# A graph layer on one core: the edge network's first product as eight small ones, some gathered rows moved to ScalarE's queue, eleven more picked tiles, another setup and end

## The chip, the cores and the metric

The kernel runs on one core of one Trainium2 chip. The metric is device time in microseconds (us). Before the change it is 1521.2 us, the median of three runs (1520.66 to 1521.42).

## What is computed

The input is a graph of N = 6250 nodes and E = 200000 edges, sorted by target node. Every edge takes the 64 features of its source node and two small vectors. Cut to what matters, the reference is:

```python
w = jax.nn.silu(edge_attr @ W1 + b1) @ W2 + b2                  # E x 32 -> E x 64 -> E x 9
h_src = features[src]                                           # a row of 64 per edge
msg = jnp.einsum('ef,em,fmg->eg', h_src, edge_sh * w, W_tp)     # E x 64
agg = jax.ops.segment_sum(msg, dst, num_segments=N) / jnp.sqrt(AVG_DEG)
emb = jax.nn.silu(c_noise[:, None] @ Wn1 + bn1) @ Wn2 + bn2     # gamma and beta of a node
gamma, beta = jnp.split(emb, 2, axis=-1)
x = layernorm(x + agg * (1.0 + gamma) + beta)
```

## The kernel before

Edges are cut into tiles of 128 (one edge per partition), and 16 tiles make a group; there are 98 groups, the last with 11 tiles. The main loop (L603 to L651) has one iteration i for each group. The order of the instructions on every engine is the order in which the program is written out (`tc.manual_schedule()`, L600), so an instruction that waits holds up all that is written behind it for the same engine.

**The rows of source nodes** come in three ways. For most tiles GpSimd issues one indirect DMA per tile (`gather`, L89, issued at L91), six groups ahead (AHEAD, seven buffers). The last three or four tiles of a group are "picked" instead (`picked`, L50, and `pick`, L463): the whole of x lies in the core's memory as two fp32r parts (`xs`), VectorE makes one-hot matrices of the row numbers (`hots`, L460), TensorE multiplies (14 products of 128x448 per tile, L475), and VectorE selects and sums (L484, L486). 355 tiles are picked, 3 in a group where 3g mod 8 is below 3 and 4 otherwise. In 16 groups (SPG) the first tile's 128 rows are fetched one by one by DMAs of SyncE's queue (`load_rows`, L98; L101 loads eight row numbers into registers, L106 issues one DMA per row, 22 rows in an iteration).

**The edge network**: `hidden(g)` (L398) makes the first layer of 2048 edges with two products of 64 rows by 128 columns by 512 (L403), each against a block-diagonal weight, into the PSUM tile p1 of two banks; one Silu (L411) reads all 1024 columns. `second(g)` (L415) makes the second layer with four 32-column products of 256 (L420) into the PSUM tile with the tag "s". `weights(g)` (L425) transposes the result (L430), multiplies (L436) and lays it out for eight target windows (`a`, L442).

**Sums**: `windows(g)` (L494) multiplies each tile's rows by its a (32 records at L504), and ScalarE copies the results from the PSUM tiles pz to zt with eight copies (L514). `project(q)` (L530), in odd iterations, multiplies two groups by W_tp (L543) into a PSUM tile pt that has p1's tag and so its place; `turn` transposes it back (L549), and `halves` reads it with ScalarE (L524) and VectorE (L525). `place` (L554) adds to nodes (L559), with a carry copied by ScalarE (L565); `bring` (L572, L576) and `finish_nodes` (L667 to L684) close 256 nodes in every fourth iteration (i mod 4 = 3), with ten operations on VectorE and a square root on ScalarE (L680). `gate` (L353) reads gamma and beta of 128 nodes from the PSUM tile "s" in iterations up to 50 (L355, L356).

The order within iteration i is: gather(i+6), loads, rows of SPG, keys(i+2) (the row numbers copied by ScalarE, L454), pick(i+1, 0) with the parts of `nodes(i)` and two one-hots strewn in, hots(i+2, 2 and 3), hidden(i+2), second(i+1), windows(i), project in odd iterations, pick(i+1, 1) with weights(i+1) and turn strewn in, picks 2 and 3. [...]

Of the kernel before, what the change touches and what calls it, by code (L numbers as in the profile page):

```python
# [15 lines left out]
P = 128  # L16
N, F, M, D, H, E = 6250, 64, 9, 32, 64, 200000
NJ = 49
# [13 lines left out]
SPR = 22  # L32
EPS = 1e-5
# [16 lines left out]
def picked(g):  # L50

    return Q - (3 * g % 8 < 3)
# [7 lines left out]
def gnn_resnorm_kernel(ctx: ExitStack, tc: tile.TileContext, x, src, dst, dst_row, ea, sh, cn,  # L60
# [18 lines left out]
    with ExitStack() as fast:  # L79
# [9 lines left out]
        def gather(g):  # L89
            hs[g] = gath.tile([P, KB, F], F32, tag="hs", name=f"hs{g}")  # L90
            hs_dma[g] = [nc.gpsimd.indirect_dma_start(  # L91
                out=hs[g][:, t - g * KB, :], out_offset=None, in_=x,
                in_offset=bass.IndirectOffsetOnAxis(ap=src_i[:, t:t + 1], axis=0))
                for t in range(g * KB + (g in SPG), g * KB + tiles(g) - picked(g))]

        src_r = keep.tile([len(SPG), P], I32)

        def load_rows(g, e0):  # L98
            for e in range(e0, min(e0 + SPR, P), 8):
                n = min(8, min(e0 + SPR, P) - e)  # L100
                _, vs = nc.values_load_multi_w_load_instructions(  # L101
                    src_r[SPG.index(g):SPG.index(g) + 1, e:e + n], engines=[mybir.EngineType.SP],
                    min_val=0, max_val=NPAD - 1,
                    skip_runtime_bounds_check_because="src is below N, as for the gathers")
                for k in range(n):
                    nc.sync.dma_start(hs[g][e + k:e + k + 1, 0, :], x[bass.ds(vs[k], 1), :])  # L106
# [27 lines left out]
        def setup(temp):  # L134
# [4 lines left out]
            for q in range(4):  # L139
                nc.sync.dma_start(w1bd[q * D:(q + 1) * D, (q % 2) * H:(q % 2 + 1) * H], w1)  # L140
            nc.sync.dma_start(src_i[:, AHEAD * KB:], src[:, AHEAD * KB:])
            xb_r = xb.rearrange("p j f -> p (j f)")
            row_i = xb_r[0:1, 0:NBLK * KB].bitcast(I32)
            nc.scalar.dma_start(row_i, dst[0:1, :])
            first_i = temp.tile([NBLK, KB], I32)
            nc.scalar.dma_start(first_i, dst[0].rearrange("(g k) -> g k", k=KB))
            cn_j = temp.tile([NJ, P], F32)
            nc.scalar.dma_start(cn_j, cn)
            for s in range(2):
                nc.scalar.dma_start(b1c[s * H:(s + 1) * H, :], b1.unsqueeze(1))  # L150
# [3 lines left out]
            for h0, h1 in ((0, 2), (2, 4), (4, 7)):  # L154
                nc.scalar.dma_start(xk[:, h0:h1, :], x_v[:, h0:h1, :])
            load(0)
            for s in range(2):
                nc.sync.dma_start(w2p[s * H:(s + 1) * H, s * M:(s + 1) * M], w2)
            nc.sync.dma_start(dst_i, dst)
# [14 lines left out]
            one = temp.tile([1, 1], F32)  # L174
            nc.vector.memset(one, 0.0)
            one_o = temp.tile([1, 1], F32)
            nc.scalar.activation(one_o, one, AF.Silu)
            row_f = xb_r[0:1, NBLK * KB:2 * NBLK * KB]
            nc.scalar.copy(row_f, row_i)
            first_t = temp.tile([NBLK, KB], F32)  # L180
            nc.scalar.copy(first_t, first_i)
# [5 lines left out]
            nc.vector.tensor_add(ident2, ident[:, 0:F], ident[:, F:P])  # L187
            zero = temp.tile([P, 1], F32)
            nc.vector.memset(zero, 0.0)
            for k in range(2):  # L190
                nc.vector.memset(ht[k][H:H + 1], 1.0)
            nc.vector.memset(wtc2[F:P, 4], 0.0)
            ones1 = temp.tile([1, P], F32)
            nc.vector.memset(ones1, 1.0)
            nc.vector.memset(eps, EPS)
            nc.vector.tensor_copy(nk, nk_i)
            nc.vector.tensor_copy(wi, n_i[:, 0:W])
            nc.vector.tensor_copy(li, n_i[:, 0:J])


            zt_r = zt.rearrange("p a c k w -> p (a c k w)")
            s_f, kp, kh, rest, t0, t1 = [zt_r[:, k * C:(k + 1) * C] for k in range(6)]
            ti = [t.bitcast(I32) for t in (t0, t1)]
            s_f = s_f.rearrange("p (g k) -> p g k", k=Q)
            nc.vector.tensor_copy(s_f[:, 0:NBLK - 1, :],
                                  src_i.rearrange("p (g k) -> p g k", k=KB)[:, 0:NBLK - 1, KB - Q:])
            nc.vector.tensor_copy(s_f[:, NBLK - 1, :], src_i[:, NT - Q:NT])
            s_f = s_f.rearrange("p g k -> p (g k)")
            nc.vector.tensor_scalar(ti[0], s_f, 2675.0, None, op0=ALU.mult)
            nc.vector.tensor_scalar(ti[0], ti[0], 17, None, op0=ALU.logical_shift_right)  # L210
            nc.vector.tensor_copy(kp, ti[0])
            nc.vector.scalar_tensor_tensor(rest, kp, -float(J * J), s_f, op0=ALU.mult, op1=ALU.add)
            nc.vector.tensor_scalar(ti[1], rest, 37.0, None, op0=ALU.mult)
            nc.vector.tensor_scalar(ti[1], ti[1], 8, None, op0=ALU.logical_shift_right)
            nc.vector.tensor_scalar(kh, ti[1], float(P), None, op0=ALU.mult)
            kf = s_f
            nc.vector.tensor_add(kf, kp, kh)
            for c0 in range(0, C, P):
                n = min(P, C - c0)
                p_kt = psum.tile([P, P], F32, tag=("s", "r")[c0 // P % 2], name=f"p_kt{c0}")  # L220
                nc.tensor.transpose(p_kt[0:n], kf[:, c0:c0 + n], ident)
                kt = t1[:, c0 // 2:c0 // 2 + P // 2].bitcast(F16)
                nc.scalar.copy(kt[0:n], p_kt[0:n])
                nc.sync.dma_start(kd[c0:c0 + n, :], kt[0:n])
            nc.vector.scalar_tensor_tensor(jl, kh, -float(J) / P, rest, op0=ALU.mult, op1=ALU.add)
            hidden(0, act=False)
            load_keys(0)
            load_keys(LB)
            for c in range(KB // 4):
                for s in range(2):  # L230
                    q = c * D + s * M
                    nc.sync.dma_start(b2c[q:q + M, :], b2.unsqueeze(1))


            rel_v = rel.rearrange("p (a b c) -> p a b c", a=2, b=2)
            dst_v = dst_i.rearrange("p (a b c) -> p a b c", a=2, b=2)
            row_v = row_f.rearrange("p (a b c) -> p a b c", a=2, b=2)

            def base(a_):
                p_b = psum.tile([P, 2, KB * P // 4], F32, tag="p1", name=f"p_b{a_}")  # L240
                for b_ in range(2):
                    nc.tensor.matmul(p_b[:, b_, 0:NBLK * KB // 4], ones1, row_v[:, a_, b_, :], start=True, stop=True)
                nc.vector.tensor_sub(rel_v[:, a_], dst_v[:, a_], p_b[:, :, 0:NBLK * KB // 4])


# [8 lines left out]
            nc.vector.tensor_copy(pw, pw_i)  # L254

            def ids():
                p_nid = psum.tile([P, NBLK], F32, tag="s", name="p_nid")
                nc.tensor.matmul(p_nid, sel, first_f, start=True, stop=True)
                nc.vector.scalar_tensor_tensor(nid, p_nid, pw, lo, op0=ALU.add, op1=ALU.subtract)

            def between(h):

                if h == 0:
                    p_f = psum.tile([KB, NBLK], F32, tag="s", name="p_f")
                    nc.tensor.matmul(p_f, first_t, ident[0:NBLK, 0:NBLK], start=True, stop=True)
                    nc.scalar.copy(first_f, p_f)
                elif h == 1:
                    keys(0)
                    hots(0, 0, Q)
                elif h == 3:  # L270
                    p_cn = psum.tile([P, NJ], F32, tag="s", name="p_cn")
                    nc.tensor.matmul(p_cn, cn_j, ident[0:NJ, 0:NJ], start=True, stop=True)
                    cn_s = temp.tile([P, NJ], F32)
                    nc.scalar.copy(cn_s, p_cn)
                    nc.sync.dma_start(cn_d, cn_s)
                    nc.sync.dma_start(wn1c, wn1.rearrange("o h -> h o"))
                    nc.sync.dma_start(bn1c, bn1.unsqueeze(1))
                    gate_load(0)
                    nc.sync.dma_start(wn2a[0:H, :], wn2)
                    nc.sync.dma_start(wn2a[H:H + 1, :], bn2.unsqueeze(0))  # L280
                    for q in range(2):
                        n = (M + 1 - q) // 2
                        nc.sync.dma_start(wtc2[q * F:(q + 1) * F, 0:n, :], wtp[:, q:M:2, :])
                    load(LB)
                    with nc.allow_non_contiguous_dma(reason="2048 words, once"):
                        nc.sync.dma_start(src_r, src[:, SPG[0] * KB:NBLK * KB:6 * KB].rearrange("p g -> g p"))
# [572 lines left out]
```

## Time and profile before

| | us |
|---|---|
| median of the runs | 1521.2 |
| the profiled execution | 1521.78 |
| its span, first to last instruction | 1519.9 |
| GpSimd's 1192 indirect DMAs: first and last start | 2.92 and 1493.22 |
| TensorE busy, of these products of the picks (L475) | 1438.0, 1090.6 |
| VectorE busy | 1135.4 |
| ScalarE busy | 526.1 |
| windows of group 0, 48, 52, 60, 96 begin (timeline, L504) | 55.8, 766.7, 825.8, 940.3, 1493.7 |

The profiled execution took 0.58 us more than the median. In the group rows of the profile a line shows the source line, the engine, the operation, the tile written and the tiles read, their shapes and the count; behind the bar are the busy time, the mean duration of one in ns, and the idle time ahead of these instructions with what ended it. In the timeline a line shows the start, the time covered (of several merged instructions the whole stretch), the engine and the instruction. PE is TensorE, PEld its weight loads, DVE VectorE, ACT ScalarE, POOL GpSimd, and SPq SyncE's queue.

### The profile page before, as it was taken

The numbers are of one execution on the slowest core, as the hardware profiler recorded it, in microseconds if no ns is written. First come the engines' busy times: TensorE is split into PE (matmuls) and PEld (weight loads), VectorE is DVE, ScalarE is ACT, GpSimd is POOL, SyncE is SP. The second block draws the span as 40 slices with busy tenths as digits, with TensorE's granted clock in tenths as the row PEclk, the third lists the DMA queues.
The fourth block names the chain that finished last, engine by engine and source line by source line (L and its number), as shares of the span: only waits on it lengthen the run. The fifth ranks groups of instructions, "written<-read, shape, count | busy, mean of one in ns | idle before, by whom it ended". The sixth has DMA issues, their size and how long they took to land.

```text
span 1519.9 us, 34363 instructions
## 1 busy us (share of the span) xinstructions
PE 1438.0 (95%) x10810; PEld 1192.7 (78%) x10810; DVE 1135.4 (75%) x1987; ACT 526.1 (35%) x1335; POOL 1129.3 (74%) x1201
## 2 busy tenths in 40 slices
PE   4998999999999999999999999989998998999995
PEld 2787888888888788888888888878777887878784
DVE  5686777877877878777777877768677777687773
ACT  4223342433423333332423424424233333333331
POOL 7777777777777777777777777777777777777772
PEclk9999999999999999999999999999999999999997
DMA  6422232222222222222322222222222222222210
GB/s 171 95 56 63 54 76 53 64 59 70 65 56 72 58 63 71 60 63 54 74 59 55 72 52 63 71 54 61 53 72 53 59 55 71 52 55 59 73 29 15
DMA packets 90939, 96.16 MB, mean 63 GB/s; under 512 B 37161, under 2 KB 51451, under 8 KB 90748
## 3 DMA queue, kind: packets, MB, share of 16 engines
q0 software_dynamic: 38144, 39.14, 13.4%
q1 hardware_dynamic: 51842, 53.09, 12.1%
q8 instruction: 88, 1.44, 0.4%
q10 hardware_dynamic: 762, 1.64, 0.3%
q14 instruction: 103, 0.84, 0.2%
HBM read 92.04 MB, written 1.73 MB: 62 GB/s over the span
## 4 chain that ended last, share of the span: by engine, by line
PE 57%; POOL 18%; issue 9%; SPq 5%; DMA 5%; DVE 4%; ACT 2%; DVEq 0%; POOLq 0%; ACTq 0%
PE px L475 41%; POOL hs L91 18%; PE pz L504 5%; DMA hs<-in_x_dram,src_i 4%; PE p L403 3%; SPq L106 3%; PE pt L543 3%; PE p L420 2%; SPq L101 2%; PE p L430 1%; PE ps L559 1%; PE ps L589 0%; ACT st L411 0%; DVE hot_k L460 0%; DVE xm L484 0%
## 5 line engine op out<-in xcount | busy, mean ns | idle before, releaser
L91 POOL DMA_INDIRECT hs<-in_x_dram,src_i x1192 | 1128.0, 946 | 364.3 <-issue 330.7
L475 PE MATMUL px<-xs,hot_k 128*128 128x448 f32 x4970 | 1090.6, 372 | 9.4 <-DVE xs L294 8.8
L475 PEld LDWEIGHTS px<-xs,hot_k 128*128 128x128 f32 x4970 | 896.8, 189 | 93.9 <-issue 10.9
L484 DVE SCALAR_TENSOR_TENSOR xm<-li,jl,px 128x448 f32<-128x448 f32 x355 | 240.3, 677 | 203.6 <-PE px L475 202.0
L460 DVE TENSOR_TENSOR hot_k<-pk,nk 128x896 fp32r<-128x896 f32 x355 | 370.6, 1082 | 3.1 <-ACT pk L454 3.1
L411 ACT ACTIVATE st<-p,b1c 128x1024 f32<-128x1024 f32 x98 | 109.5, 1118 | 405.4 <-PE p L403 405.1
L486 DVE TENSOR_REDUCE hs<-xm 128x64 f32<-128x448 f32 x355 | 220.1, 620 | 12.2
L514 ACT COPY zt<-pz 64x160 f32<-64x160 f32 (+2 forms) x784 | 213.5, 272 | 40.6 <-PE pz L504 28.0
L504 PEld LDWEIGHTS pz<-a,hs 128*64 128x64 f32 x3126 | 110.2, 142 | 68.1 <-issue 61.2
L504 PE MATMUL pz<-a,hs 128*64 128x72 f32 x3126 | 124.6, 234 | 27.0 <-DMA hs<-in_x_dram,src_i 11.5
L442 DVE TENSOR_TENSOR a<-oh,p 128x1152 f32<-128x1152 f32 x98 | 132.7, 1354 | 3.3
L436 DVE TENSOR_TENSOR p<-p,sh 128x72 f32<-128x72 f32 x196 | 47.0, 240 | 100.9 <-ACT rt L546 45.2
L403 PE MATMUL p<-ea,w1bd 64*128 64x512 f32 x392 | 113.3, 655 | 0.0
L565 ACT COPY carry<-ps 128x128 f32<-128x128 f32 x48 | 12.8, 266 | 273.4 <-PE ps L559 273.4
L420 PEld LDWEIGHTS p<-st,w2p 128*32 128x32 f32 x784 | 15.8, 108 | 83.2 <-issue 39.0
L420 PE MATMUL p<-st,w2p 128*32 128x256 f32 x784 | 63.5, 396 | 7.8 <-DVE xb L356 7.8
L680 ACT ACTIVATE var<-var,eps 128x2 f32<-128x2 f32 (+1 forms) x25 | 7.4, 295 | 179.2 <-DVE var L679 179.2
L543 PE MATMUL pt<-zt,wtc 128*64 128x128 f32 x960 | 64.3, 281 | 2.6 <-ACT zt L514 1.7
L543 PEld LDWEIGHTS pt<-zt,wtc 128*64 128x64 f32 x960 | 55.0, 142 | 3.8 <-ACT zt L514 1.9
L454 ACT CAST pk<-kr 128x384 f32<-128x384 f16 (+1 forms) x98 | 53.8, 549 | 2.2 <-DMA kr<-kd 2.2
L430 PE MATMUL p<-ident,p2s 128*128 128x128 f32 x196 | 53.3, 273 | 0.0
L403 PEld LDWEIGHTS p<-ea,w1bd 64*128 64x128 f32 x392 | 30.0, 187 | 28.7 <-issue 28.0
(122 smaller groups left out, 529.0 us busy)
## 6 DMA issues: line engine op xcount, KB each, us to landing
hs<-in_x_dram SPq DMA_DIRECT2D x2048, 0.2 KB
ea<-in_ea_dram SPq DMA_DIRECT2D x49, 512.0 KB
hs<-in_x_dram,src_i POOLq DMA_INDIRECT x1192
kr<-kd SPq DMA_DIRECT2D x49, 256.0 KB
sh<-in_sh_dram SPq DMA_DIRECT2D x49, 144.0 KB
cb<-cn_d SPq DMA_DIRECT2D x12, 128.0 KB
out_dram<-o SPq DMA_DIRECT2D x24, 64.0 KB
gam<-in_x_dram ACTq DMA_DIRECT2D x2, 448.0 KB
```

The lines of the kernel that those rows point to most:

```text
L91: hs_dma[g] = [nc.gpsimd.indirect_dma_start(out=hs[g][:, t - g * KB, :], out_offset=None, in_=x, in_offset=bass.IndirectOffsetOnAxis(ap=sr ...
L403: nc.tensor.matmul(p1[:, i, :], w1bd[i * 64:(i + 1) * 64, :], e[i * 64:(i + 1) * 64, :], start=True, stop=True)
L411: nc.scalar.activation(st[g], p1_t.pop(g), AF.Silu, bias=b1c)
L420: nc.tensor.matmul(p2[g][c * D:(c + 1) * D, 0, :].rearrange("p (i e) -> p i e", i=2), w2p, s[:, :, c * P:(c + 1) * P], start=True, stop=True)
L442: nc.vector.tensor_mul(a[g], oh_t.pop(g)[:, :, None, :].to_broadcast([P, KB, M, W]), sw.unsqueeze(3).to_broadcast([P, KB, M, W]))
L460: nc.vector.tensor_tensor(hot_k[g, t], pk_t[g][:, t, None, :].to_broadcast([P, J, P]), nk.unsqueeze(2).to_broadcast([P, J, P]), op=ALU.is_ ...
L475: nc.tensor.matmul(px.rearrange("p f l -> p (f l)"), hot_k[g, t][:, h, :], xs[i][:, h].rearrange("p f l -> p (f l)"), start=(h == 0 and i ...
L484: nc.vector.scalar_tensor_tensor(xm, li[:, None, :].to_broadcast([P, F, J]), jl[:, c:c + 1], px, op0=ALU.is_equal, op1=ALU.mult)
L486: nc.vector.tensor_reduce(hs[g][:, tiles(g) - q + t, :], xm, AX.X, ALU.add)
L504: mm = nc.tensor.matmul(pz[v * F:(v + 1) * F, k // 2].rearrange("p m w -> p (m w)"), hsg[:, k0 + k, :], ag[:, k0 + k].rearrange("p m w -> ...
L514: nc.scalar.copy(z[h * F:(h + 1) * F, 0:5 - h, k0 + v:k0 + n:2, :].rearrange("p m k w -> p k m w"), pz[v * F:(v + 1) * F, 0:(n + 1 - v) // ...
L543: nc.tensor.matmul(pt[h * F:(h + 1) * F, 0, 0:P], wtc2[:, c, :], z[h][:, c], start=(c == 0), stop=(c == 4))
```

## The change

1. **First layer.** `hidden(g)` makes eight products of 32 rows by 64 columns by 256 (four row parts q, two column parts s) in place of two. They go to four banks: the two of p1, half used, and the two of pz, which `windows` uses too. Three Silu instructions (256, 256 and 512 columns) read them. hidden(i+2) moves from behind pick(i+1, 0) to behind pick(i+1, 1). L420 and L436 read their operands in the new arrangement; their counts and sizes stay.
2. **ScalarE's rows.** In seven groups (16, 28, ... 88; ACG) the first tile's 128 rows come one by one from ScalarE's queue, 11 in each of the twelve iterations before, behind hidden(i+2); the indirect DMA of that tile goes.
3. **Picks.** `picked` is 3 where g mod 4 = 0 and in the last group, 4 otherwise: 366 tiles. 1174 indirect DMAs are left.
4. **Setup.** x is loaded first and in four pieces; it is split with one ScalarE copy per part in place of two; the row numbers of groups 0 and 1 are spread by a product on TensorE, and only those of the later groups take the way through DRAM; most of the other small steps come after the first picks.
5. **End.** The last three picks, project and place come ahead of the last windows; the last group's windows run in reverse order with four PSUM banks, and ScalarE and VectorE share the copies; the store of finished nodes is issued at the start of the next iteration.

The diff, cut to its core:

```diff
 def picked(g):
-    return Q - (3 * g % 8 < 3)
+    return Q - (g % 4 == 0 or g == NBLK - 1)
...
+ACG = range(16, NBLK, 12)
+ACR = 11
...
-                for t in range(g * KB + (g in SPG), g * KB + tiles(g) - picked(g))]
+                for t in range(g * KB + (g in SPG or g in ACG), g * KB + tiles(g) - picked(g))]
...
+            if g in SPG:
+                eng, kind, n1, to = nc.sync, mybir.EngineType.SP, SPR, hs[g][:, 0, :]
+            else:
+                eng, kind, n1, to = nc.scalar, mybir.EngineType.Activation, ACR, hs_r[ACG.index(g) % 2]
...
                 for k in range(n):
-                    nc.sync.dma_start(hs[g][e + k:e + k + 1, 0, :], x[bass.ds(vs[k], 1), :])
+                    eng.dma_start(to[e + k:e + k + 1, :], x[bass.ds(vs[k], 1), :])
...
-        def hidden(g, act=True):
+        def hidden(g):
             e = ea_t.pop(g)
-            p1 = psum.tile([P, 2, KB * P // 4], F32, tag="p1", name=f"p1_{g}")
-            for i in range(2):
-                nc.tensor.matmul(p1[:, i, :], w1bd[i * 64:(i + 1) * 64, :], e[i * 64:(i + 1) * 64, :],
-                                 start=True, stop=True)
...
-            nc.scalar.activation(st[g], p1_t.pop(g), AF.Silu, bias=b1c)
+            p1 = psum.tile([P, 2, 4 * P], F32, tag="p1", name=f"p1_{g}")
+            bank = [p1[:, i, 0:2 * P] for i in range(2)]
+            bank += [psum.tile([P, 2 * P], F32, tag="pz", name=f"p1_{g}_{i}", bufs=2) for i in range(2)]
+            for q in range(4):
+                eq = e[q * D:(q + 1) * D, :].rearrange("p (c s e) -> p s c e", s=2, e=P)
+                for s in range(2):
+                    nc.tensor.matmul(bank[q][s * H:(s + 1) * H].rearrange("p (c e) -> p c e", e=P),
+                                     w1bd[q * D:(q + 1) * D, (q % 2) * H:(q % 2 + 1) * H], eq[:, s],
+                                     start=True, stop=True)
+            st[g] = work.tile([P, 4, 2 * P], F32, tag="st", name=f"st{g}")
+            nc.scalar.activation(st[g][:, 2], bank[2], AF.Silu, bias=b1c)
+            nc.scalar.activation(st[g][:, 3], bank[3], AF.Silu, bias=b1c)
+            nc.scalar.activation(st[g][:, 0:2], p1[:, :, 0:2 * P], AF.Silu, bias=b1c)
...
-                if i + 2 < NBLK:
-                    hidden(i + 2)
                 if i + 1 < NBLK:
                     second(i + 1)
-                if i < NBLK - 2:
+                if i < NBLK - 1:
                     windows(i)
-                turn = project(i // 2) if i % 2 == 1 else []
+                turn = project(i // 2) if i % 2 == 1 and i < NBLK - 1 else []
...
                 if i + 1 < NBLK:
                     pick(i + 1, 1, [weights(i + 1), turn])
+                if i + 2 < NBLK:
+                    hidden(i + 2)
+                for g in ACG:
+                    if 0 < g - i <= 2 * AHEAD:
+                        load_rows(g, (2 * AHEAD - g + i) * ACR)
+                if i == NBLK - 2:
+                    sums(i + 1)
+                    turn = project(i // 2)
+                    ps = psum.tile([P, 2 * P], F32, tag="s", name="ps_l")
+                    pick(i + 1, 2, [turn])
+                    more = place(i // 2, ps)
...
+            def split(h):
+                xh = gam[:, h * J:(h + 1) * J, :].rearrange("p l f -> p f l")
+                nc.scalar.copy(xs[0][:, h], xh)
+                nc.vector.tensor_sub(xs[1][:, h], xh, xs[0][:, h].bitcast(F32))
```

## The prediction

> **What bounds the kernel now.** I read the busy times first, then the costliest groups, then the timeline of single iterations. From the page, parts 1 and 5:
>
> ```profile
> PE 1438.0 (95%) x10810; PEld 1192.7 (78%) x10810; DVE 1135.4 (75%) x1987; ACT 526.1 (35%) x1335; POOL 1129.3 (74%) x1201
> ...
> L91 POOL DMA_INDIRECT hs<-in_x_dram,src_i x1192 | 1128.0, 946 | 364.3 <-issue 330.7
> L475 PE MATMUL px<-xs,hot_k 128*128 128x448 f32 x4970 | 1090.6, 372 | 9.4 <-DVE xs L294 8.8
> ...
> L403 PE MATMUL p<-ea,w1bd 64*128 64x512 f32 x392 | 113.3, 655 | 0.0
> ```
>
> TensorE looks full and GpSimd three quarters full, yet GpSimd never rests: 1128.0 busy and 364.3 idle, 0.30 behind each gather, make 1.25 us per gather from 2.92 to 1494.2, without one wait. Both engines are close to the bound. Which one it is shows in the distance between the end of a group's last gather and its windows (timeline): 36 us for group 0, 13 for group 48, about 1.6 (the landing) from group 62 on. TensorE starts late, is faster, and from there waits for gathers. Up to group 48, at 766.7, nothing of that; groups 52 to 60 take (940.3 - 825.8)/8 = 14.31 us. Unhindered, group 96 would begin at 766.7 + 48 x 14.31 + 5.6 (two picks ahead of it) = 1459.2, not 1493.7. So **GpSimd ends last, and TensorE has 34.5 us to spare**: alone it would give a span of 1485.4.
>
> The timeline, in iteration 47 (the first three lines) and 95 (the last), both of which close nodes:
>
> ```profile
> 750.88 1.13 PE L403 MATMUL p<-ea,w1bd 64*128 64x512 f32 x4
> 752.77 0.64 PE L420 MATMUL p<-st,w2p 128*32 128x256 f32 x8 [0.77 <-DVE xb L356]
> 759.60 0.28 DVE L525 TENSOR_TENSOR r<-pt,r 128x128 fp32r<-128x128 f32 x1
> ...
> 1478.30 0.28 DVE L525 TENSOR_TENSOR r<-pt,r 128x128 fp32r<-128x128 f32 x1
> ```
>
> Call E the time at which pick(i+1, 0) is through (750.88; 1470.24 in iteration 95). The first layer stands at E and covers the wait of L420 for the gate, which ends at E + 1.89. VectorE works without a gap from the node sums to L525, and reads the last of pt at E + 9.0, in iteration 95 at E + 8.3. Today nobody waits for that.
>
> **What the Trainium skill says.** "TensorEngine Tiling (Array Packing)", Tiling Modes: 32x64 gives eight tiles that work independently; changing the mode drains the array. The trace agrees as far as it goes: L420's four column parts, eight records of 379 ns, take 0.64 us together. "TensorE: Matmul & The Clock Gate", Measured speedup vs the span model: 6.32 times for nine tiles in rows and columns; no run here shows both ways at once. "Perfetto Trace Analysis", Per-engine timelines: ScalarE and VectorE run in strict order, and an instruction waits for its semaphores in a queue; the trace agrees, ScalarE's sequencer passing L524 only as that starts. "DMA: Bandwidth & Descriptors", Issuing engines are not separate DMA queues: a second queue saves issue time alone. SyncE's rows show that time:
>
> ```profile
> L101 SPq TENSOR_LOAD <-src_r x288: 691/996/2056, 52.0 to 1482.6; - x144
> L106 SPq DMA_DIRECT2D hs<-in_x_dram x2048: 224/228/313, 57.0 to 1484.0; - x187
> ```
>
> Start to start a row costs 0.41 us.
>
> **The change part by part**, against the span 1519.9 (the execution took 1521.78, so 1.9 lies around it; it is 0.58 above the median).
>
> *Gathers.* Eleven more picks and seven ScalarE groups take 18 of 1192: 18 x 1.25 = 22.5 us off GpSimd. Its first needs only the first load of row numbers, as now. It ends at 1494.2 - 22.5 = 1471.7; with today's 25.7 us behind it, 1497.4.
>
> *Picks.* 14 products at 0.200 (40 in 8.01 on the chain of waits) are 2.80: 11 x 2.80 = +30.8 on TensorE. VectorE gets 11 x (0.677 + 0.620 + 1.082) = 26 us on 1135; it has the room.
>
> *First layer.* Now 1.06 from L403's start to L420's. The eight products have half the columns, as L420's have (256): taken at L420's slot, 0.57 (723.49 to 724.06). Bounds: 0.46 (half of the present products' 0.91 at 512 columns, without any fill) and 1.15 (no overlap in one direction, or a drain on either side). Gain 98 x 0.49 = -48.0, bounds -59 and +9. The three Silu take about 0.46 + 0.46 + 0.6 for 1.12: +0.4 on ScalarE at 35%, hidden by its idle time.
>
> *Where it moves to.* Three things. (a) In the 11 closing iterations up to 47 the wait of L420 loses its cover: 11 x 1.06 = +11.7. (b) hidden(i+2) writes p1, which is pt's place, so in odd iterations TensorE waits for L525, and picks 2 and 3 are queued behind it. Where no nodes close, L525 would end near E + 6.1, as TensorE arrives at E + 0.57 (L420) + 2.24 (windows, project) + 3.14 (pick) = 5.95: at most 0.2, left out. In closing iterations up to 47 it arrives at 1.85 + 5.95 = 7.8 and waits to 9.0: 11 x 1.2 = +13; in the 12 after, 5.95 against 8.35: 12 x 2.4 = +29. Bounds 0 and 60 for (b): VectorE could be ahead or later. (c) pz is free in time: the eight copies end at T + 3.2 (T the start of the windows), hidden comes at T + 4.2 or later: nothing; without that cover, some tenths.
>
> *ScalarE's rows.* By SyncE's price 11 x 0.41 + 2 x 1.0 = 6.5 us in each of the iterations 4 to 87, behind the Silu. Queued behind: keys(i+2), the carry, the square root, p2s. ScalarE has 526 us of work, 5.4 an iteration, and 14.6 to do it in; so 12.3 fit. No gain is possible, as work is added. Bounds: 0, and 42 (third rival). Taken at 0. Their landing, about 2 us, has most of an iteration.
>
> *SyncE.* It gets the deferred stores, one issue of 0.4 us in four iterations, and loses the stall of a store that waits for its node sums: nothing.
>
> *Setup.* ScalarE's splitting of x goes from 14 copies of 0.9 to 7, and groups 0 and 1 skip the way through DRAM (transposes at 12.38, keys landed at 21.5). Picks of group 0 begin some 10 us earlier than at 25.7. VectorE is what the setup then waits for: from 3 us on about 3 for keys of two groups, 2 for spreading them, 7 differences of 0.63, 7 one-hots of 1.08, 3 selections of 1.3, 2.3 for the first weights, and some 4 of waits for TensorE, an estimate: to about 30. The steps for the other keys (4.9, from 7.83 to 12.8 today) end at 35; TensorE's small products follow, and with pick(1, 0), 2.8, and L420 group 0's windows come at about 42 instead of 55.8. The later keys land 9.1 us behind the 35, at 44; hots(2) waits for them on VectorE, and behind it the selection of pick(1, 0), whose bank pick(1, 2) wants: some 2 are given back. -11.5, bounds -4 and -18. POOL is not touched.
>
> *End.* Two picks (5.6) leave the stretch ahead of the last windows but one and come behind it; the copies of the last windows (1.95) are shared: -4, bounds -7 and 0.
>
> Sum on TensorE: 1485.4 + 30.8 - 48.0 + 11.7 + 42 - 11.5 - 4 = 1506.4, above GpSimd's 1497: **TensorE becomes the bound**, with 1506.4 + 1.9 = 1508; the end's gain counts on GpSimd's side too. I take 1507.
>
> **Rivals.** *GpSimd stays the bound:* if (a) and (b) cost under some 42 instead of 54, the gathers decide: 1497.4 with about 2 of the end's gain, plus 1.9: 1497. For it: it never rests. *TensorE gets waits not priced here,* 0.15 us an iteration (px, one-hots late): 1507 + 15 = 1522, no change. *Slower, by ScalarE's rows:* in a closing iteration hidden ends at E + 9.6, the rows at 16.1, keys 0.6 and the carry 0.27 follow, VectorE's sum and gate 0.65, so "s" is free for L420 at E + 17.8. TensorE, with one pick of that light group (3) left, is there at 9.6 + 2.8 + 3.3 = 15.7: 2.1 late, 20 times (7 to 83) = 42: 1549. It decides from a burst above 4.4 us. For it: SyncE's price; against it: every link must be in series at full price. *The eight products don't run side by side:* slot 1.06 or more, 1507 + 48 = 1555.
>
> **How the numbers follow.** Forecast 0.42; GpSimd 0.22; unpriced waits 0.09; ScalarE 0.22; no overlap 0.05. Faster by over 0.2% (what a measurement can tell here; below 1518.2): 0.64; within: 0.09; slower: 0.27. The range 1493 to 1545 reaches from GpSimd's case to most of ScalarE's; below it lies 0.05, above some 0.13. Cases of one sign hold most of the chance.
>
> **What would show it.** Eight products within 0.6 us (L403's successor); TensorE waiting for VectorE's reading of pt ahead of them in closing iterations by 1.2 and 2.4; gathers ending near 1472, and the distance to the windows at 20 to 35 us to the end (it shrinks to 1.6 if GpSimd's case holds). ScalarE's case shows as L420 waiting for carry or gate in iterations 8, 12, ... 84. Wrong if the slot is 1 us, or if the first windows aren't near 42.

## The result and the profile after

The changed kernel takes 1697.3 us (median of four, 1689.3 to 1700.7), the kernel before on the same chip 1521.0: a ratio of 1.1155 (1.1135 to 1.1175). It is 176 us slower where 14 us of gain were predicted. The profiled execution, the fastest of the four, took 1689.3 (span 1687.5).

Parts 1 and 5 of its page:

```profile
PE 1488.8 (88%) x12145; PEld 1237.3 (73%) x12145; DVE 1163.9 (69%) x2041; ACT 572.3 (34%) x1517; POOL 1114.2 (66%) x1183
...
L93 POOL DMA_INDIRECT hs<-in_x_dram,src_i x1174 | 1112.9, 948 | 466.4 <-issue 315.9
...
L417 PE MATMUL p<-ea,w1bd 32*64 32x256 f32 x1568 | 69.9, 413 | 51.4 <-DVE r L542 49.5
```

No engine is full. TensorE's work grew by 51 us only, its span by 168. GpSimd, which hardly waited before, now has 102 us more of idle time: the gathers wait for buffers that TensorE gives back late. So the bound is a wait. The table of waits names it (engine, line, releaser: us, times, longest):

```profile
POOL hs L93 <- PE pz L520: 115.8, 38, 7.3
DVE yt L586 <- ACT carry L583: 112.0, 42, 5.9
...
PE p L432 <- DVE xb L363: 63.8, 34, 5.0
...
PEld p L432 <- ACT carry L583: 46.9, 22, 5.4
```

Before, VectorE waited 8.2 us in all for the carry:

```profile
DVE yt L568 <- ACT carry L565: 8.2, 25, 1.0
```

Now it is 112.0, in 42 iterations: ScalarE, busy for 34% of the span, is late. The timeline of one even iteration shows the chain (all engines in order of time; other lines left out):

```profile
1125.45 0.47 ACT L421 ACTIVATE st<-p,b1c 128x256 f32<-128x256 f32 x1 [3.03 <-PE p L417]
...
1127.69 4.14 ACTq L116 DMA_DIRECT2D hs_r<-in_x_dram  x7
...
1131.92 0.59 ACT L466 CAST pk<-kr 128x512 f32<-128x512 f16 x1 [5.05 <-DMA hs_r<-in_x_dram]
1132.44 0.26 ACT L583 COPY carry<-ps 128x128 f32<-128x128 f32 x1
1132.73 0.29 DVE L586 TENSOR_TENSOR yt<-ps,carry 128x128 f32<-128x128 f32 x1 [2.64 <-ACT carry L583]
...
1133.08 0.64 PE L432 MATMUL p<-st,w2p 128*32 128x256 f32 x8 [1.65 <-DVE yt L586]
```

The Silu, then the row burst (here the last seven of a group), then the row numbers of the picks (L466), and only then the carry. The node sums (L586) wait for the carry, and TensorE's second layer (L432) waits for both, since they hold the PSUM tile "s" that it writes. The 1.65 us is no work of anybody; it is a place in ScalarE's queue. L466's releaser names the rows' transfer, as the latest event; L466 does not need those rows, it stood behind their issue.

### The profile page after: what moved, and what is told of

Read it like the earlier page. It is cut to its first block, busy times and chain, and to the rows that moved or that the text cites. A ratio compares the mean times of both kernels' runs of the same rounds, so it can differ in the third digit from the quotient of the medians.

```text
span 1687.5 us, 40238 instructions
## 1 busy us (share of the span) xinstructions
PE 1488.8 (88%) x12145; PEld 1237.3 (73%) x12145; DVE 1163.9 (69%) x2041; ACT 572.3 (34%) x1517; POOL 1114.2 (66%) x1183
## 3 DMA queue, kind: packets, MB, share of 16 engines
q10 hardware_dynamic: 2368, 1.84, 0.4%
## 4 chain that ended last, share of the span: by engine, by line
PE 38%; SPq 20%; issue 10%; DVE 9%; ACTq 9%; DMA 6%; ACT 6%; POOL 2%; DVEq 0%; POOLq 0%
PE px L487 25%; SPq L116 11%; SPq L111 8%; ACTq L116 6%; PE pz L520 5%; PE p L432 3%; ACTq L111 3%; PE p L417 2%; DVE hot_k L472 2%; DMA hs<-in_x_dram 2%; POOL hs L93 2%; DVE a L454 2%; DMA kr<-kd 2%; ACT pk L466 2%; PE pt L561 1%
## 5 line engine op out<-in xcount | busy, mean ns | idle before, releaser
L93 POOL DMA_INDIRECT hs<-in_x_dram,src_i x1174 | 1112.9, 948 | 466.4 <-issue 315.9
L487 PE MATMUL px<-xs,hot_k 128*128 128x448 f32 x5124 | 1172.9, 379 | 2.5 <-ACT xs L244 1.3
L487 PEld LDWEIGHTS px<-xs,hot_k 128*128 128x128 f32 x5124 | 934.1, 192 | 132.2 <-issue 43.0
L496 DVE SCALAR_TENSOR_TENSOR xm<-li,jl,px 128x448 f32<-128x448 f32 x366 | 247.3, 676 | 296.0 <-PE px L487 295.7
L472 DVE TENSOR_TENSOR hot_k<-pk,nk 128x896 fp32r<-128x896 f32 x366 | 381.7, 1081 | 16.9 <-ACT pk L466 14.7
L466 ACT CAST pk<-kr 128x512 f32<-128x512 f16 (+1 forms) x96 | 54.2, 564 | 554.6 <-DMA hs_r<-in_x_dram 332.6
L531 ACT COPY zt<-pz 64x160 f32<-64x160 f32 (+1 forms) x780 | 212.5, 272 | 32.8 <-PE pz L520 23.5
L432 PE MATMUL p<-st,w2p 128*32 128x256 f32 x784 | 68.4, 422 | 102.7 <-DVE xb L363 63.8
L421 ACT ACTIVATE st<-p,b1c 128x256 f32<-128x256 f32 x98 | 46.5, 474 | 205.7 <-PE p L417 200.9
L432 PEld LDWEIGHTS p<-st,w2p 128*32 128x32 f32 x784 | 17.0, 111 | 134.5 <-ACT carry L583 46.9
L417 PE MATMUL p<-ea,w1bd 32*64 32x256 f32 x1568 | 69.9, 413 | 51.4 <-DVE r L542 49.5
L435 ACT ACTIVATE p2s<-p,b2c 128x256 f32<-128x256 f32 x98 | 46.3, 473 | 174.1 <-PE p L432 174.1
L586 DVE TENSOR_TENSOR yt<-ps,carry 128x128 f32<-128x128 f32 x47 | 13.7, 291 | 112.0 <-ACT carry L583 112.0
L417 PEld LDWEIGHTS p<-ea,w1bd 32*64 32x64 f32 x1568 | 23.5, 133 | 83.9 <-DVE r L542 68.8
L423 ACT ACTIVATE st<-p,b1c 128x512 f32<-128x512 f32 x98 | 67.6, 690 | 0.0
```

The source lines that it names most:

```text
L93: hs_dma[g] = [nc.gpsimd.indirect_dma_start(out=hs[g][:, t - g * KB, :], out_offset=None, in_=x, in_offset=bass.IndirectOffsetOnAxis(ap=sr ...
L432: nc.tensor.matmul(p2[g][c * D:(c + 1) * D, 0, :].rearrange("p (i e) -> p i e", i=2), w2p, s[:, c // 2::2, c % 2 * P:(c % 2 + 1) * P], sta ...
L472: nc.vector.tensor_tensor(hot_k[g, t], pk_t[g][:, t, None, :].to_broadcast([P, J, P]), nk.unsqueeze(2).to_broadcast([P, J, P]), op=ALU.is_ ...
L487: nc.tensor.matmul(px.rearrange("p f l -> p (f l)"), hot_k[g, t][:, h, :], xs[i][:, h].rearrange("p f l -> p (f l)"), start=(h == 0 and i ...
L496: nc.vector.scalar_tensor_tensor(xm, li[:, None, :].to_broadcast([P, F, J]), jl[:, c:c + 1], px, op0=ALU.is_equal, op1=ALU.mult)
L531: (nc.vector.tensor_copy if end and v else nc.scalar.copy)(z[h * F:(h + 1) * F, 0:5 - h, k0 + v:k0 + n:2, :].rearrange("p m k w -> p k m w ...
```

## The experiments

Groups 28 to 48 took 14.63 us each before and 17.10 after; groups 52 to 60 took 14.31 and 17.01 (starts of the windows, timeline). With most runs below the same two numbers stand, first for groups 28 to 48, then for 52 to 60. The theories of the cause: **S**, ScalarE's queue is held by the rows; **F**, the first layer's new form and place; **O**, picks, setup and end; later **C** and **D**.

**One part undone or done alone.** Four kernels first ran on a chip on which the kernel before itself took 2519 us at a mean clock of about 0.8. Their ratios, in the order of the texts that follow, were 1.009, 1.053, 1.013 and 1.034. Part 2 alone is the slowest there as it is later, but nothing below rests on these four.

> The changed kernel with part 2 undone: no rows from ScalarE's queue, and the seven tiles are gathered by GpSimd again (1181 gathers). Theory S (ScalarE's in-order queue is held about 8 us in each of 84 iterations by the rows, so that keys, carry, square root and p2s are late and TensorE waits): about 1533 us; the iterations 88 to 95, which have no rows, took 14.85 us on average and show what the others would take. Theory F (the first layer's new form and place cost the time, through p1 and pz): stays near 1690. Theory O (picks, setup and end): stays near 1690 as well.

> The kernel before with part 2 alone: the first tile of seven groups row by row from ScalarE's queue, written behind pick(i+1, 1). Theory S: slower by 60 to 160 us (1580 to 1680); TensorE has 34 us to spare, and 84 iterations lose 1.2 to 2.2 us each. Theories F and O: seven gathers fewer at 1.25 us, so 1512 to 1521.

> The kernel before with part 1 alone: eight small products and hidden(i+2) behind pick(i+1, 1). Theory S together with the prediction's terms for this part (-48 for the slot, +12 and +42 for the waits): TensorE alone would give 1491, GpSimd's 1192 gathers still end last, so 1519 to 1523. Theory F: 1640 to 1690.

> The changed kernel with a smaller burst in the same iterations: one register load and six rows instead of two loads and eleven rows, so about 4.4 us instead of 8.2 of ScalarE's queue; five rows of eleven of the first tile in the seven groups are left out (their part of the buffer holds zeros). Theory S with the threshold that the prediction named (a burst above 4.4 us decides): most of the loss is gone, 1533 to 1570. If the cost went with the number of rows fetched (transfers), about 1533 + 6/11 of 155, so 1618. If a register load behind the Silu were enough by itself, above 1640.

The same kernels on a chip like the first one:

*Part 2 undone.*

```diff
-ACG = range(16, NBLK, 12)
+ACG = range(0)
```

> The changed kernel without the rows from ScalarE's queue once more, since the first four kernels ran on a chip on which the kernel before itself took 2519 us. Theory S: about 1533 us. Theories F (first layer) and O (picks, setup and end): near 1690.

Measured: 1562.2, ratio 1.0248 (1.0231 to 1.0265; the kernel before took 1523.6 on this chip); 15.39 and 15.33 us a group. So the rows cost 135 of the 176 us. S was right in kind; F and O fall as main causes, though 55 us against the prediction's 1507 remain for them. VectorE's waits for the carry are down to 7.2 us (first line). The others are what is left on TensorE:

```profile
DVE yt L586 <- ACT carry L583: 7.2, 24, 0.3
...
PEld p L417 <- DVE r L542: 53.4, 47, 2.5
...
PEld p L432 <- ACT var L705: 23.1, 11, 2.2
PE p L432 <- DVE xb L363: 19.3, 11, 1.8
```

*Part 2 alone*, in the kernel before: ACG, hs_r and load_rows as in the change, called behind pick(i+1, 1).

> The kernel before with part 2 alone: the first tile of seven groups row by row from ScalarE's queue, written behind pick(i+1, 1). Theory S: slower by 60 to 160 us (1580 to 1680), as TensorE has 34 us to spare and 84 iterations lose 1.2 to 2.2 us each. Theories F and O: seven gathers fewer, so 1512 to 1521.

Measured: 1693.0, ratio 1.1129 (1.1110 to 1.1147); 17.09 and 17.09. This part by itself makes a loss as large as the whole, more than S had said. It doesn't take quite the same way, though, for the waits show a second one:

```profile
ACT pk L466 <- DMA hs_r<-in_x_dram: 369.6, 55, 8.1
...
PEld p L415 <- DMA ea<-in_ea_dram: 144.4, 36, 6.5
...
SPq L116 <- DMA hs_r<-in_x_dram: 251.6, 86, 9.7
```

TensorE's first layer waits for edge features here, which it does neither in the kernel before nor in the changed one. SyncE issues them 4.0 us ahead of their use (median) in place of 14.5, as its own rows stand still for up to 9.7 us (86 waits, 252 us) while ScalarE's are on their way. In the trace the transfers of both queues name the same eight completion semaphores (100 and 102 to 108), and each waits for its own semaphore ahead of its issue, that is, until the earlier transfer that used it has landed. So the two queues wait for each other: theory **C**.

*Part 1 alone*, in the kernel before: the new hidden, second and weights, hidden(i+2) behind pick(i+1, 1).

> The kernel before with part 1 alone: eight small products, and hidden(i+2) behind pick(i+1, 1). By the prediction's terms (1485.4 - 48 + 12 + 42 on TensorE) GpSimd stays the bound: 1519 to 1523, with TensorE's windows of group 48 at about 767. Theory D (at its new place the first layer no longer stands next to the second; every change between the large products and small ones costs 0.29 us of drain on TensorE, and there is one more of them in each iteration, 28 us in all): TensorE alone would give some 1518, group 48 comes about 10 us later (777), and the time is 1520 to 1532. Theory F (this part costs most of the 176 us): 1640 to 1690.

Measured: 1533.4, ratio 1.0081 (1.0065 to 1.0098); 14.99 and 14.98; from group 0 to 48 727.0 us for 710.9 before. F falls. The prediction's terms had this part change TensorE by +6 in all; it is slower than that. It also lies just above D's range: D's estimate was 10 us for these 48 groups, and 16 came.

*Half the burst.*

```diff
-            for e in range(e0, min(e0 + n1, P), 8):
-                n = min(8, min(e0 + n1, P) - e)
+            for e in range(e0, min(e0 + n1, P), 8 if g in SPG else ACR):
+                n = min(8 if g in SPG else 6, min(e0 + n1, P) - e)
```

> The changed kernel with a smaller burst in the same iterations: one register load and six rows instead of two loads and eleven rows, about 4.4 us of ScalarE's queue instead of 8.2. Five rows of eleven of the first tile in the seven groups are left out (their part of the buffer holds zeros). Theory S with the threshold that the prediction named (a burst above 4.4 us decides): nearly all of the 135 us is gone, 1560 to 1585. If the cost goes with the number of rows fetched: 1562 + 6/11 of 135, so about 1636. If a register load behind the Silu is enough by itself: above 1650.

Measured: 1560.9, ratio 1.0272 (1.0252 to 1.0292); 15.34 and 15.24. The burst lasts 4.1 us (mean, first register load to last issue) in place of 7.8, and costs nothing against the run without rows. The cost is no price per row: there is room for a short burst.

**Which of the two holds, S or C.**

*ScalarE's rows without SyncE's:* `SPG = range(0)`, with the seven ACG groups as they are.

> The changed kernel with ScalarE's rows as they are, but without SyncE's rows: the first tile of the sixteen SPG groups is gathered by GpSimd (1190 gathers). In the trace of the kernel before with part 2 alone, SyncE's rows stop for up to 5 us while ScalarE's rows are on their way, and TensorE waits for loads of edge features that SyncE issues late. Theory C (the rows of the two queues wait for each other, since all such transfers share eight completion semaphores in turn and each waits for the one eight before it to have landed; the pair needs 17 us an iteration): without SyncE's rows the loss is gone, 1555 to 1590. Theory S (ScalarE's own queue, held about 8 us by its two register loads and eleven issues, is enough): 1650 to 1697.

Measured: 1652.3, ratio 1.0883 (1.0844 to 1.0921); 16.51 and 16.10. Some 90 us stay, 45 go. The burst's mean falls from 7.80 to 7.31 us: 84 x 0.49 = 41. The stops of SyncE's rows that the text names last up to 9.7 us, not 5, as shown above. So C takes part, in that it lengthens the burst, and S carries two thirds (16 more gathers are in this kernel; GpSimd's last starts at 1538, 78 us ahead of group 96, and doesn't decide).

*The hold without transfers.*

```diff
+                if 4 <= i < 88:
+                    for k in range(21):
+                        nc.scalar.copy(scr, scr)
```

> The changed kernel without rows on ScalarE's queue, but with 21 copies of 128x256 there in the same iterations (4 to 87), which hold ScalarE for about 7.8 us at the same place and touch no transfer. Theory S: 1640 to 1700. Theory C: the hold alone costs at most the 42 us that the prediction's third rival worked out, 1562 to 1605.

Measured: 1916.6, ratio 1.2597 (1.2576 to 1.2618); 19.60 and 19.38. A held ScalarE is sufficient, with no transfer of rows at all (the lines stand two further down in this kernel, L588 for L586):

```profile
DVE yt L588 <- ACT carry L585: 170.0, 43, 6.5
...
PE p L434 <- DVE xb L365: 133.5, 34, 5.6
```

The time lies above even S's range, because the copies hold ScalarE longer than meant. The mean time from the end of the Silu to the end of what follows it is 9.0 us here (8.5 of them copies) and 6.5 in the changed kernel, whose first register load runs beside the Silu; it is 6.0 without SyncE's rows and 2.8 with six rows. Against the 1562 without rows these four cost 354, 135, 90 and -1 us. Between 6.0 and 9.0 each us costs some 87, about 1 us in each of the 84 iterations; a line through these three reaches zero near 5 us, which is an estimate. The copies slow no other engine's work: VectorE's three operations of the picks take 1081, 676 and 620 ns, as without them.

*The link.* Everything as changed, but the carry copied by VectorE:

```diff
-                        nc.scalar.copy(carry[q], pd[:, P:2 * P])
+                        nc.vector.tensor_copy(carry[q], pd[:, P:2 * P])
```

> The changed kernel, rows on ScalarE's queue and all, with one edit: the copy of the carry is made by VectorE, not by ScalarE, where it stands behind the rows and the row numbers of the picks. Theory S with the carry as its decisive link (the PSUM tile with the tag s is free for the second layer only after carry, node sums and gate; this holds in every even iteration, 42 times, not in 20): most of the 75 us that the second layer waits more than without the rows is gone and with it the half clock that follows each wait, so 1575 to 1625. If the row numbers (keys), the square root or p2s behind the rows are what counts: 1660 to 1700.

Measured: 1629.6, ratio 1.0726 (1.0707 to 1.0745); 15.86 and 15.88. This lies between the two forecasts: half of the 135 us go through the carry. The second layer now waits no more than without the rows (46 us for 43, and 118 in the changed kernel; counted as the time over 0.20 us from the weight load ahead to its first weight load, without the first groups). The other half has moved to the next thing behind the burst, the row numbers:

```profile
DVE hot_k L472 <- ACT pk L466: 94.8, 48, 5.0
```

It was 14.7 with the carry on ScalarE. That this explains the remaining 67 us is read from the trace; no run moved both.

**The other parts, and a better version.**

*The first layer at its old place,* without ScalarE's rows: hidden(i+2) again ahead of second(i+1).

> The changed kernel without the rows from ScalarE's queue and with hidden(i+2) back at its old place, just ahead of second(i+1); the eight small products stay. Theory D with the waits of the prediction: the waits for VectorE's reading of pt (38 us), the longer wait of the second layer (10 us) and the drain (28 us) go, against a wait of windows for the first two Silu of some 0.3 us an iteration (they share pz): TensorE alone would give about 1515 and the 1181 gathers 1511, so 1508 to 1522, and an iteration between groups 28 and 48 takes 14.3 to 14.9 us instead of 15.4. Without theory D, 20 to 28 us later: 1535 to 1545.

Measured: **1508.5, ratio 0.9917 (0.9900 to 0.9933)**; 14.83 and 14.50. It beats both kernels, the one before by 0.8%, which is clear of the noise. GpSimd ends last, 1181 gathers, as at first. That the time lies near the predicted 1507 is chance: there TensorE was to decide. The reading of pt and one drain are gone, and the windows' wait for the Silu comes in, smaller:

```profile
PEld pz L520 <- ACT st L421: 61.8, 90, 1.6
```

*Picks alone:* `picked` of the change in the kernel before.

> The kernel before with part 3 alone, 366 picks in place of 355. By the prediction's terms TensorE alone comes to 1485.4 + 30.8 = 1516 in span and GpSimd to 1519.9 - 11 x 1.25 = 1506: 1515 to 1521, as TensorE becomes the bound. If a pick costs less than 2.8 us where TensorE waited for gathers: 1507 to 1512.

Measured: 1520.8, ratio 1.0002 (0.9993 to 1.0011); 15.05 and 14.66; profiled span 1516.5. No difference: eleven picks move the bound from GpSimd to TensorE and no more (the windows now begin 17 us or more behind the last gather of their group to the end). They pay only beside a cheaper first layer.

*Two tries at more,* both with the gate ahead of the closing of nodes on VectorE (e12: hidden behind pick(i+1, 2), 373 picks; e14: hidden at its old place, 370 picks).

> A version meant to beat both: the changed kernel without ScalarE's rows, hidden(i+2) behind pick(i+1, 2) (no wait for VectorE's reading of pt), the gate ahead of the closing of nodes on VectorE (no wait of the second layer for the ten closing operations), and seven more picked tiles (373; groups 68, 72, ... 92 take four). From the run with hidden at its old place (1508.5; GpSimd last): GpSimd ends 7 x 1.25 = 8.8 earlier; TensorE would begin group 96 at 1470 - 12 (wait for the gate) - 8 (the windows' wait for the Silu, less one drain) + 19.6 (picks) = 1470. Theory D with these terms: 1498 to 1508. If the waits come back in another place: 1515 or more.

> The version with hidden at its old place (1508.5), with the gate ahead of the closing of nodes on VectorE and four more picked tiles (370). GpSimd's last gather comes 4 x 1.25 = 5 us earlier, which gives 1503; TensorE unhindered would begin group 96 near 1470 + 11 (picks) less up to 12 (the wait for the gate), so it doesn't decide: 1500 to 1507. If the gate's wait doesn't go, TensorE decides: 1508 to 1513.

Measured: 1517.1, ratio 0.9973 (0.9965 to 0.9982), and 1531.9, ratio 1.0067 (1.0049 to 1.0086). e12 misses its range and lands in its alternative; e14 misses both. In e14 the second layer's wait for the gate is indeed gone, but the square root of the closing stands in ScalarE's queue ahead of the Silu and waits for VectorE, and the windows wait for the Silu: in closing iterations up to 47 1.84 us more than in others (2.26 for 0.42). The wait that was taken away had been 1.17 (in the version at 1508.5, 1.49 for 0.32). Such an iteration takes 0.9 us more than in the version at 1508.5, and behind six of the eleven TensorE's clock is halved once (1.6 us each): about 20 us up to group 48.

```profile
PEld pz L520 <- ACT st L421: 82.6, 95, 2.4
...
PE pz L520 <- ACT st L421: 34.5, 23, 1.9
```

In e12 TensorE decides to the end (group 96 at 1485, not 1470). It has one wait that the version at 1508.5 has only once, that of the picks' products for VectorE's selection (L487 for L496: 15.3 us in 23 waits); whether this makes the 15 us was not tested.

## Why the prediction was wrong

**The step that failed is "ScalarE's rows ... Taken at 0".** It compared ScalarE's load with the time of an iteration ("5.4 an iteration, and 14.6 to do it in; so 12.3 fit"). That is an average, and what counts is which instruction stands behind the burst and when its result is wanted. The slower rival of the prediction had the right chain, but at 42 us a third of the size of 135. Its threshold, a burst of 4.4 us, isn't contradicted (4.1 cost nothing), though the dearer runs point to one nearer 6 (5 us behind the Silu and the 1.3 that the burst runs beside it). What this rival had wrong:

- *The burst was 7.8 us, not 6.5.* The register loads took 2.0 and 1.0 us, the rows 0.39 each, and the waits for SyncE's rows about 0.5 (C; 7.3 without these rows).
- *It acts in 42 iterations, not in 20.* The prediction counted closing iterations. The carry is copied in every even one (L583), and "s" waits for it in all of them. From the windows of group g to the next, by g mod 4 and from group 60 to 84, the changed kernel needs 14.63, 17.95, 14.94 and 19.99 us, without the rows 14.18, 15.84, 14.65 and 16.64: two of four lose 2.1 and 3.4.
- *A wait costs more than its length.* The two layers' waits grew by 90 us (second 43 to 118, first 63 to 78). The mean clock fell from 0.974 to 0.954: 1562.8 x 0.026 = 41 us against 1687.5 x 0.046 = 78. Together they make 127 us, and the two spans differ by 125.

**The rest, 1562 for 1507,** by the prediction's own terms:

- *GpSimd ends last, 34.5 us spare on TensorE:* right. The picks alone came to a span of 1516.5 in the profiled execution, the fastest of twelve (median 1519.0), where 1485.4 + 30.8 = 1516 was said. The distance between the gathers and the windows is 1.5 to 6.5 us from group 62 to 95, where the prediction read about 1.6.
- *Slot 0.57:* 0.62 (52 to 60: 4.96 us for eight groups). The eight products do run side by side; that rival falls. +5.
- *The move's drain* was not priced, though the prediction cited the Trainium skill, "TensorEngine Tiling (Array Packing)", Tiling Modes, that a change of mode drains the array. The trace agrees: the weight load of a small product starts 0.49 us behind that of the large one ahead of it, not 0.20. At its old place the first layer shares this with the second; at the new one each has its own: 98 x 0.29 = 28 us.
- *(a):* 1.79 us in the eleven closing iterations against 0.76 before, +11 for +11.7. *(b):* +0.78 and +2.10 for 1.2 and 2.4, and 0.18 in other odd iterations, 38 us for 42. *(c):* nothing at the new place, as said; at the old one 0.37 us a group (52 to 60), within "some tenths".
- *Setup -11.5:* no gain that shows. Group 0's windows begin at 55.1, not near 42 (54.2 without the rows; on chips like the first one 52.4 to 56.8 in all runs with the new setup, 52.7 to 55.8 with the old one). VectorE's first chain ended at 37.3, not 30. TensorE ran at half clock from 27.6 to 34.4 us and from 41.2 to 54.9, so that pick(1, 0) took 5.60 us for 2.8. Its second layer of group 0 waited 4.58 us. The view names no releaser, but the new setup puts the row numbers of group 1 into the PSUM tile "s", which the second layer then overwrites, and the wait ends just as the last of VectorE's one-hots of group 1, which read them, is done (29.18). From the timelines of VectorE and TensorE in the changed kernel:

```profile
26.10 3.08 DVE L472 TENSOR_TENSOR hot_k<-pk,nk 128x896 fp32r<-128x896 f32 x3
...
29.39 1.08 PE L432 MATMUL p<-st,w2p 128*32 128x256 f32 x8 [4.58 <-issue]
...
48.78 5.60 PE L487 MATMUL px<-xs,hot_k 128*128 128x448 f32 x14
```

- *End -4:* about -2.4 (28.9 us behind the start of group 96's windows, against 25.7 with the picks alone plus the two picks moved there, 5.6).
- *The clock's share,* which the prediction left out: without the rows 41 us are lost to it, where the kernel before lost 26.

In the order of the list these are 5 for the slot, 28 for the drain, -5 for (a) and (b), 10 for the setup, 2 for the end and 15 for the clock: 55 of 55. That the sum comes out so well is in part luck. These terms are read from traces, the setup's lies within its scatter from run to run, and the clock's is a difference of means that may overlap the setup's.

## What to carry to other kernels

The busy share of an engine doesn't tell whether more work fits on it. List what stands behind the new work in its queue, who waits for each of these, and in how many iterations, and make the burst no longer than the shortest such slack (here 4.1 us were free and 7.8 cost 135 us in all). DMA issues and register loads hold a compute engine's queue as work does, while the profile does not count them as busy. A step of small products that is moved away from another such step pays for its own change from large products to small ones (here 0.29 us).

## What the runs showed of the hardware

Behind most waits of TensorE of some 2 us or more its clock is halved for a few us. The same two groups of instructions are shown here behind a wait of 2.42 us, and then without one in another closing iteration:

```profile
713.56 1.05 PE L432 MATMUL p<-st,w2p 128*32 128x256 f32 x8 [2.42 <-DVE xb L363]
714.54 2.19 PE L520 MATMUL pz<-a,hs 128*64 128x72 f32 x32
```

```profile
1115.38 0.64 PE L432 MATMUL p<-st,w2p 128*32 128x256 f32 x8
1115.94 1.22 PE L520 MATMUL pz<-a,hs 128*64 128x72 f32 x32
```

Between 130 and 1540 us the changed kernel has 26 such stretches of half clock, 3.4 or 6.8 us each, 116 us together. All 26 begin 2.1 to 5.2 us behind the start of one of TensorE's 36 idle stretches of 1.9 us or more; behind its 46 idle stretches of 0.3 to 1.9 us none begins. Without the rows there are 13 stretches of half clock, 11 of them behind waits of 2.1 us or more and two behind waits of 1.75. The kernel before has 6 with 43 us, of which one at its end makes 22.

A load of up to eight row numbers into registers took from 0.74 to 2.0 us on ScalarE's queue, and a row's issue 0.39 us there against 0.41 on SyncE's.
